# Two layers of a vision network on one core: the last gate moved ahead of the gather, four factors kept in PSUM, and the residual addition given to GpSimd

## The chip, the core and the metric

The kernel runs on one core of a Trainium2 chip. A core has five engines that run their own instruction streams in order and wait for one another through semaphores: TensorE (PE: matrix products and transposes, from SBUF into PSUM), VectorE (DVE), ScalarE (ACT), GpSimd (POOL) and SyncE (SP, which here issues most DMA transfers). SBUF holds the operands, 128 partitions wide; PSUM holds the results of PE in eight banks of 512 float32 columns. Everything is float32.

The metric is the device time of one execution in microseconds (us), lower is better. Times stand for one profiled execution, or for the median of separate runs, and the text says which.

## The reference

The input x is 4 x 48 x 48 x 128 (images, height, width, channels). Two layers run one after the other, each as `x = x + layer(group_norm(x))`.

```python
# layer 0: four scan directions over the 2304 pixels of an image
xz = einsum('bhwc,ec->bhwe', x, in_proj_w); xin, z = split(xz, 2)
xc = silu(depthwise_conv3x3(xin) + conv_b)
xs = stack([x0, x1, x0[..., ::-1], x1[..., ::-1]])     # rows, columns, and both reversed
dt = softplus(dts + dt_proj_b)
h = h * exp(dt_l * A) + (dt_l * u_l) * B_l             # a scan over pixels, 16 states
y = einsum('bkdn,bkn->bkd', h, C_l)
y = (sum of the four directions + Ds * xs)
y = (y - mean(y)) * rsqrt(var(y) + 1e-5) * norm_g + norm_b
out = einsum('bhwd,cd->bhwc', y * silu(z), out_proj_w)

# layer 1: attention and two spectral convolutions over "images" of 48 x 128
xa_n = _inorm(xa)
k, q, v = _fno_layer(xa_n, ...) three times            # rfft2, weights on low modes, irfft2, plus a scaled skip
out = softmax(q k^T / sqrt(d)) v ; projd = _fno_layer(out, wP, ...)
attention = _inorm(projd + xa)
an = _inorm(attention)
m = gelu(_inorm(spec_conv(an, wM0)) + skip(an))
m = _inorm(spec_conv(m, wM1)) + skip(m)
output = _inorm(m) + attention
```

`_inorm` subtracts the mean of an image and divides by its standard deviation. `group_norm` does so over groups of four channels.

## The kernel before

**Order.** Nearly all compute operations are issued through a helper, `Ordered`, that keeps the order of the program on each engine; so they all have line L55 in the profile, and groups are told apart by tile names. Transfers are issued by SP in program order. Code that belongs beside other code is written as Python generators that are advanced piece by piece: where a generator yields, something else is issued.

**Layer 0** (`first_layer`) goes through images 0 to 3, through four directions each, through five chunks each (four of 480 pixels, one of 384), and through 16 steps per chunk, one for each state. A step scans on VectorE (`h`), multiplies by C on GpSimd (`hc`) and sums on PE (`yp`). `put_away` runs when a step's sums are through; after a chunk's last step (`u.i == N - 1`) it copies the sums (`turned`) and queues a `gather`, which adds the directions (`pg`, into `yb`) and queues `back` for the chunk (L487 to L561). `back` is a chain: mean `pm`, subtraction, `Square` on ScalarE, `pv` on PE, a power -0.5 on GpSimd (`var`), transpose `pe`, factor `rs`; then the gate, two products `pz` with two ScalarE operations each and one product on VectorE giving silu(z) (kept in `z`); then `yb *= z` on GpSimd, projection `po`, times `rs`, a second projection `pr` of z with the input added, and the final sum. For the last chunk (image 3, pixels 0 to 479) the result goes straight into `x_in[1]`, the copy of images 2 and 3 that layer 1 reads.

**Between the layers**, that last `back` runs in turn with `opening` (L1131 to L1194): pieces of the one, then pieces of the other. `opening` loads layer 1's constants and x_in (seven transfers, L1161), and for images 0 and 1 (pair 0, still in SBUF as `x_0`) takes statistics (`measure`, which is BATCH_NORM_STATS), the scale and shift (`affine`, with two small PE products and a power on GpSimd), the `means`, the forward spectra along the width (`forward_w`: twelve products `pa`, evacuated in turn by VectorE and ScalarE) and the variances (`squares`, with `pv`, to the factor `in_r`). Once the last chunk is there ("done"), it takes the last statistics and the scale of pair 1 (images 2 and 3). Pair 1's means and spectra come in the gather phase of layer 1 (L1437 to L1446).

**Layer 1's last part** works on two `Strand`s (L1875 to L2245), strand 0 for images 0 and 1, strand 1 for images 2 and 3; y is the strand's 48 rows of 128 x 96 (attention), m the same for the two spectral convolutions. Each strand has main phases p0 to p5 and tails t0 to t5. The loop at the end issues p0(strand 0), p0(strand 1), p1(strand 0) and so on, and with each step of a phase two steps of the tail of the phase before it, which is one of the other strand. What matters here:

- p2: spectra along the height (`e_m`), stored to DRAM; beside them GpSimd computes `m = y * sw`, six operations of 768 columns a strand (the profile calls y `xa`).
- t2: loads the spectra back (`load_e2`, L1932), sums, and the factor `t3 = rsqrt(...) * s2`: a Sqrt on ScalarE, a reciprocal and the product `t<-t,s` on VectorE.
- p3: in each pair of steps `e_m *= t3`, then inverse transforms on PE (`pi_m`), `m += pi_m`, GELU and Square on ScalarE, sums on PE into the tile `st`; GpSimd computes `y *= s1` (`xa<-xa,s`), six of 768 columns.
- p4: spectra again, their squares on ScalarE and products `ce = e * a2` on VectorE, both summed on PE; GpSimd adds the input to y (`xa<-xa,xr`).
- t4: the factors `v5`, `s5`, `qe`, `qm` on vectors of 96 columns (t, v, d, s, sw in the profile).
- p5: `e_m *= qe`, then `skip`: `m *= qm` and `m += y`, two operations each of 768 columns; then `pi_m` on PE and `m += pi_m`; then `put`: transposes on PE (`pf`), a copy with bias on ScalarE (`ot`) and the store. `put(t - 1)` is issued in step t, `put(5)` in t5.

Each strand's sums tile `st` is a PSUM bank opened anew in phases p1 to p4 (`open_sums`); sums fill 384 of its 512 columns. All the factors are tiles of 96 columns in SBUF.

Of the kernel before, what the change touches and what calls it, by code (L numbers as in the profile page):

```python
# [10 lines left out]
F32 = mybir.dt.float32  # L11
BF16 = mybir.dt.bfloat16
AF = mybir.ActivationFunctionType
# [45 lines left out]
def first_layer(ctx, tc, io, x1_dram, sp_dram, d_w, d_m, opening):  # L59
# [426 lines left out]

    def back(b, s, n, yb, x, w, wb):  # L487
# [70 lines left out]
        if b == B - 1 and s == 0:  # L558
            to = images[b]["x1"][:, 1].rearrange("w h t -> w (h t)")[:, 0:n]
# [158 lines left out]
    def gather(c, yt):  # L718

        k, s, n = c.k, c.s, c.n  # L720
        final = k == ORDER[-1]
        if final:
            yb = two.tile([128, NF, LC], F32, tag="yb", name=f"yb{c.t}")
        elif "y" not in c.im:
            c.im["y"] = one.tile([128, NF, L], F32, tag="y", name=f"y{c.b}")
        for f in range(NF):
            p = side(f"pg{c.t}_{f}")
            if final:
                w, v = ident, c.im["y"][:, f, s : s + n]
            else:  # L730
                w, v = ddiag[:, f], c.im["xc"][:, f, s : s + n]
            for j, t in enumerate((yt, c.old)):
                for q, r in blocks(n):
                    on.tensor.matmul(
                        p[:, q * LB : q * LB + r],
                        t[0:r, q, f * 128 : (f + 1) * 128],
                        ident[0:r, 0:r],
                        start=(j == 0 and q == 0),
                        stop=False,
                        is_transpose=True,  # L740
                        skip_group_check=True,
                    )
            on.tensor.matmul(p[:, 0:n], w, v, start=False, stop=True, skip_group_check=True)
            yield
            if final:
                on.scalar.copy(yb[:, f, 0:n], p[:, 0:n])
            else:
                on.scalar.copy(at(c.im["y"], 1, s, n)[:, f], like(p[:, 0:n], 1))
            if f == 0:
                yield FREE  # L750
        if c.next:
            recall(c.next)
        if final:
            backs.append(back(c.b, s, n, yb, c.im["x"], c.im["w"], c.im["wb"]))
            later.append(backs[-1])

    def put_away(u):

        c, n = u.c, u.c.n
        if u.i < N - 1:  # L760
            return
# [29 lines left out]
    later, backs, gathers, projected = deque(), deque(), deque(), deque()  # L791
# [190 lines left out]
def layer1(ctx, tc, io, x1_dram, out):  # L982
# [78 lines left out]
    def spread(psum, p, t, name, aff=None):  # L1061

        v = small.tile([128, T], F32, tag="in_s", name=f"in_{name}{p}")
        on.vector.tensor_reduce(v, t[:, 0 : HB * T].rearrange("p (h t) -> p t h", t=T), AX.X, ALU.add)
        o = psum.tile([128, 512], F32, tag="st", name=f"po_{name}{p}")
        for b in range(2):
            ob = o[:, b * T : (b + 1) * T]
            on.tensor.matmul(ob, g_of[:, b], v, start=True, stop=aff is None)
            if aff is not None:
                on.tensor.matmul(ob, aff[:, 1, b : b + 1].to_broadcast([128, 128]), over_w, start=False, stop=True)  # L1070
        return o

    def means(psum, p, x, aff):
# [3 lines left out]
        pm = psum.tile([128, 512], F32, tag="st", name=f"pm{p}")  # L1077
# [10 lines left out]
        om = spread(psum, p, pm, "m", aff)  # L1088
# [42 lines left out]
    def opening(stack, x_0, last):  # L1131
# [31 lines left out]
        measure(0, 0, x_0, range(6))  # L1163
        yield
        measure(0, 1, x_0, range(6))
        yield
        made["aff"] = [affine(psum, 0)]
        yield
        trans = forward_w(psum, work, 0, x_0, made["aff"][0])
        norm = means(psum, 0, x_0, made["aff"][0])  # L1170
        for _ in range(3):
            next(norm)
            yield
        made["m"] = next(norm)
# [5 lines left out]
        for i in range(5):  # L1180
            next(rest)
            yield
            if i == 1:
                measure(1, 0, x_in[1], range(6))
        made["r"] = [next(rest)]
        measure(1, 1, x_in[1], range(2, 6))
        over_h = const.tile([H, H], F32, name="over_h")
        nc.gpsimd.memset(over_h, 1.0 / H)
        ident = load("ident1", [128, 128], io["c_ident"])
        fh = load("fh", [96, 96], io["c_FH"])  # L1190
        while "done" not in last:
            yield
        measure(1, 1, x_in[1], range(2))
        made["aff"].append(affine(psum, 1))  # L1194
# [193 lines left out]
    with ExitStack() as ph:  # L1388
# [51 lines left out]
        norm = means(psst, 1, x_in[1], aff[1])  # L1440
        trans = forward_w(psum, work, 1, x_in[1], aff[1])
        for _ in range(3):
            next(norm)
        next(trans)
        m = next(norm)
        mine = squares(psst, work, 1, x_in[1], aff[1], m)  # L1446
# [429 lines left out]
    class Strand:  # L1876


        def __init__(self, p):
            self.p = p  # L1880
            self.y = xa[:, :, p * P : p * P + P]
            self.m = None
            self.e2 = {}

        def bank(self, name):
            return psum.tile([128, 512], F32, tag="mm", name=f"{name}_{self.p}")

        def open_sums(self, name):
            self.st = psst.tile([128, 512], F32, tag=f"st{self.p}", name=f"st_{name}_{self.p}")
# [25 lines left out]
        def rsqrt(self, name, v, bias, scale=1.0):  # L1915
            r = self.vector(name)
            on.scalar.activation(r, v, AF.Sqrt, bias=bias, scale=scale)
            on.vector.reciprocal(r, r)
            return r
# [29 lines left out]
        def along_h(self, name, fill, more=None, beside=None):  # L1949
            self.de = dram.tile([2, H, 32, P], F32, name=f"de_{name}_{self.p}")  # L1950
            self.wait = []
            for k in range(0, 32, 4):
# [6 lines left out]
                on.scalar.copy(e[:, k % 8 : k % 8 + 4], images(b[0:96]))  # L1959
                if k % 8 == 4:  # L1960
# [7 lines left out]
        def product(self, e, other, k0, name):  # L1968
            t = self.blk("ap", [128, 8, P], f"{name}{k0}", 4)[0:96]
            if other is None:  # L1970
                on.scalar.activation(t, e, AF.Square)
            else:
                on.vector.tensor_mul(t, e, other)
# [53 lines left out]
        def p1(self):  # L2027

            self.open_sums("y")
# [35 lines left out]
        def p2(self):  # L2065

            self.m = imgs.tile([128, H, P], F32, tag=f"p{self.p}", name=f"m_{self.p}")
            self.open_sums("m0")
# [5 lines left out]
            def more(e, k0):  # L2074
                n = k0 // 8
                t = self.product(e, None, k0, "sqe0")
# [9 lines left out]
        def t2(self):  # L2086
# [6 lines left out]
            self.t3 = self.rsqrt("t3", self.s22, eps)  # L2093
# [3 lines left out]
        def p3(self):  # L2097

            self.open_sums("g")
# [39 lines left out]
        def p4(self):  # L2139

            self.open_sums("m1")
# [4 lines left out]

            def more(e, k0):
                ts = [self.product(e, None, k0, "sqe1"), self.product(e, self.a2[:, k0 : k0 + 8], k0, "ce1")]
# [13 lines left out]
            yield from self.along_h("m1", fill, more, beside)  # L2162

        def t4(self):
# [9 lines left out]
            v5, u = self.vector("v5"), self.vector("d")  # L2174
# [6 lines left out]
            s5 = self.rsqrt("s5", v5, eps)  # L2181
            self.times(s5, s5, n_g[:, 5:6])
            yield
            self.qe, self.qm = self.vector("t3"), self.vector("sw")
            self.times(self.qm, s5, wsm[1])
            on.vector.tensor_mul(self.qe, t4, s5)
# [19 lines left out]
        def p5(self):  # L2206


            def skip(q):
                for i in range(2):  # L2210
                    v = self.m[:, 24 * i + q : 24 * i + q + 8]
                    on.vector.tensor_mul(v, v, over(self.qm, 8))
                    on.vector.tensor_add(v, v, self.y[:, 24 * i + q : 24 * i + q + 8])

            for t in range(6):
                q = 8 * (t // 2)
                if t % 2 == 0:
                    on.vector.tensor_mul(self.e2[q], self.e2[q], over(self.qe, 8))
                    skip(q)
                for b, h in self.along_w("m1", t):  # L2220
                    v = self.m[:, h : h + QB]
                    on.vector.tensor_add(v, v, images(b))
                if t:
                    self.put(t - 1)
                yield

# [142 lines left out]
```

## Time and profile before

| what | us |
|---|---|
| median of three runs | 4452.84 (4444.05, 4452.84, 4453.03) |
| the profiled execution | 4458.8 |
| its span, first to last instruction | 4457.0 |
| VectorE busy, PE busy | 3865.2 (87%), 3808.3 (85%) |
| ScalarE busy, GpSimd busy | 3440.9 (77%), 3351.2 (75%) |
| mean granted PE clock | 0.947 of full speed |

The span falls into layer 0's scans (to about 3710), the passage between the layers and the attention (to about 4190), and the strands' phases. The following view gives the engines' busy time in six stretches of the span (start:end, length, then busy us of each engine with its number of instructions; PEclk is the granted PE clock, the last two are the share of time that the DMA engines were busy and what they moved):

```profile
0.00:3700.00 3700.00, 3192.94 (x22270) 2619.96 (x22271) 3400.54 (x2115) 3158.00 (x6459) 3025.03 (x3217) 0.96 0.36 101
3700.00:3820.00 120.00, 79.84 (x327) 37.06 (x324) 57.16 (x110) 26.49 (x45) 28.90 (x128) 0.82 0.33 90
4190.00:4290.00 100.00, 87.04 (x531) 56.08 (x530) 19.23 (x46) 43.33 (x93) 20.68 (x26) 0.85 0.51 136
4290.00:4314.00 24.00, 2.67 (x25) 1.78 (x23) 23.93 (x3) 4.29 (x6) 23.60 (x14) 0.63 0.28 77
4314.00:4400.00 86.00, 65.93 (x392) 32.70 (x392) 38.01 (x68) 50.08 (x93) 16.62 (x9) 0.76 0.63 146
4400.00:4457.00 57.00, 33.60 (x166) 19.86 (x166) 45.88 (x65) 18.28 (x32) 6.69 (x3) 0.77 0.47 133
```

The engines stand in the order PE, PE's weight loads, VectorE, ScalarE, GpSimd.

### The profile page before, as it was taken

What the parts mean: (1) busy time and instruction counts of PE and PEld (TensorE: products, weight loads), DVE (VectorE), ACT (ScalarE), POOL (GpSimd) and SP (SyncE); (2) the same over time, 40 slices, a digit from 0 to 9 for tenths busy, and PEclk for the clock granted to TensorE, in tenths of its full rate; (3) what the DMA queues carried; (4) which work ended last, traced back from release to release, by engine and by line L of the source; (5) the groups of instructions that cost most, each with busy time, mean ns of one, the idle gap of its engine ahead of it and who ended that gap; (6) DMA issues with size and microseconds to landing.
All of it is one profiled execution on the core that took longest, in us unless ns stands there. A gap on an engine that the chain in (4) does not pass through costs nothing. (4 is left out here: it accounts for less than half of the span.)

```text
span 4457.0 us, 73318 instructions
## 1 busy us (share of the span) xinstructions
PE 3808.3 (85%) x26040; PEld 2932.0 (66%) x26040; DVE 3865.2 (87%) x2652; ACT 3440.9 (77%) x6963; POOL 3351.2 (75%) x3515
## 2 busy tenths in 40 slices
PE   6989987888899978898999788878887796989866
PEld 3767776777677767776777677766776673534434
DVE  3989899999898999998999999998999995578546
ACT  3888888998788889987888898888999883424344
POOL 2777788988787889887778898887888984258432
PEclk9999999999899999998999999999999998999987
DMA  2333333433333333333333334334333333147536
GB/s 62 92 97 100 96 94 102 115 100 107 97 102 94 94 103 107 107 106 97 102 96 98 100 113 122 108 102 102 104 107 100 107 99 100 51 108 170 131 100 163
DMA packets 327946, 463.13 MB, mean 104 GB/s; under 512 B 112772, under 2 KB 295492, under 8 KB 326876
## 3 DMA queue, kind: packets, MB, share of 16 engines
q1 hardware_dynamic: 313072, 435.81, 35.7%
q10 hardware_dynamic: 14508, 22.64, 1.5%
q8 instruction: 206, 3.38, 0.3%
q14 instruction: 160, 1.31, 0.1%
HBM read 403.10 MB, written 55.44 MB: 103 GB/s over the span
## 5 line engine op out<-in xcount | busy, mean ns | idle before, releaser
L55 POOL TENSOR_TENSOR hc<-h,cbc 128x960 f32<-128x960 f32 (+1 forms) x1280 | 2546.4, 1991 | 563.0 <-PE yp L55 184.0
L55 DVE TENSOR_TENSOR_SCAN h<-da,carry,db 128x962 f32<-128x962 f32 (+1 forms) x640 | 1358.2, 2122 | 114.9 <-ACT da L55 95.5
L55 DVE TENSOR_TENSOR_SCAN h<-decay,carry,da 128x962 f32<-128x962 f32 (+1 forms) x640 | 1365.2, 2133 | 7.0 <-PE da L55 5.5
L55 PE MATMUL yp<-ident,hc 128*128 128x128 f32 (+1 forms) x9728 | 1263.2, 282 | 57.0 <-POOL hc L55 53.4
L55 PEld LDWEIGHTS yp<-ident,hc 128*128 128x128 f32 (+1 forms) x9728 | 1133.6, 144 | 222.8 <-issue 110.2
L55 ACT ACTIVATE scaled<-turned,bt 128x256 f32<-128x256 f32 (+1 forms) x2432 | 1037.2, 499 | 28.3 <-ACT turned L55 23.6
L55 ACT ACTIVATE da<-dt,a_neg 128x480 f32<-128x480 f32 (+1 forms) x1280 | 826.9, 646 | 187.3 <-DVE h L55 164.5
L55 ACT ACTIVATE decay<-dt,a_neg 128x480 f32<-128x480 f32 (+1 forms) x1280 | 800.2, 675 | 28.4 <-DVE h L55 23.9
L55 PE MATMUL da<-ident,scaled 128*128 128x128 f32 (+1 forms) x4864 | 647.2, 276 | 196.4 <-DVE h L55 180.8
L55 DVE TENSOR_TENSOR db<-du,pb 128x960 f32<-128x960 f32 (+1 forms) x640 | 701.3, 1096 | 110.4 <-PE pb L55 100.6
L55 PEld LDWEIGHTS da<-ident,scaled 128*128 128x128 f32 (+1 forms) x4864 | 544.3, 145 | 245.6 <-ACT scaled L55 100.0
L55 PE MATMUL pb<-ident,bt 128*128 128x128 f32 (+1 forms) x2432 | 375.7, 276 | 37.2 <-DVE db L55 37.1
L55 PEld LDWEIGHTS pb<-ident,bt 128*128 128x128 f32 (+1 forms) x2432 | 292.2, 141 | 169.3 <-issue 98.9
L55 PE MATMUL pc<-pad,w_c 128*128 128x480 f32 (+1 forms) x720 | 336.5, 582 | 6.5 <-ACT th L55 3.0
L55 POOL TENSOR_TENSOR du<-dt,xc 128x480 f32<-128x480 f32 (+1 forms) x160 | 206.3, 1290 | 49.9 <-ACT dt L55 49.9
L1769 PE MATMUL acc<-v,attn_c 128*64 128x384 f32 x1152 | 203.0, 492 | 9.1 <-DVE v L1751 5.4
L55 PEld LDWEIGHTS da<-carry,ident 128*128 128x128 f32 x1280 | 201.6, 199 | 0.0
L55 PE MATMUL da<-carry,ident 128*128 128x2 f32 x1280 | 197.7, 224 | 0.0
L55 POOL COPY carry<-h 128x2 f32<-128x2 f32 x1024 | 194.3, 190 | 0.0
L1753 POOL TENSOR_TENSOR v<-grep,xrep 128x768 f32<-128x768 f32 x88 | 162.7, 1852 | 35.1 <-PE acc L1769 23.3
L55 PE MATMUL pd<-xd,w_dt 40*128 40x480 f32 (+1 forms) x320 | 172.1, 619 | 16.7 <-ACT bt L55 7.8
L1751 DVE TENSOR_TENSOR v<-gp,xrep 128x1536 f32<-128x1536 f32 x88 | 153.7, 1754 | 27.6 <-PE acc L1769 12.4
(395 smaller groups left out, 3863.5 us busy)
## 6 DMA issues: line engine op xcount, KB each, us to landing
cbc<-cd SPq DMA_DIRECT2D x512, 240.0 KB
cbc<-other SPq DMA_DIRECT2D x512, 240.0 KB
xrep<-dxt SPq DMA_DIRECT2D x44, 576.0 KB
cbc<-cd SPq DMA_DIRECT2D x128, 192.0 KB
cbc<-other SPq DMA_DIRECT2D x128, 192.0 KB
yt<-turned ACTq DMA_DIRECT2D x40, 384.0 KB
old<-yt SPq DMA_DIRECT2D x40, 384.0 KB
grep<-dgt SPq DMA_DIRECT2D x16, 576.0 KB
```

Source lines behind the costliest of these rows:

```text
L55: return lambda *args, **kw: self._tc.keep_in_program_order(emit(*args, **kw))
L1751: nc.vector.tensor_mul(v, gp[:, None, :, 0:NC].to_broadcast([128, 2, 2, NC]), x[:, :, 0:2])
L1753: nc.gpsimd.tensor_mul(v3, r[:, 2:3].to_broadcast([128, 2, NC]), x[:, :, 2])
L1769: nc.tensor.matmul(acc[c][64 * b : 64 * b + 64, 0:NC], attn_c[:, 2 * pair + b, g, q], v[:, b, c] if c < 2 else v3[:, b], start=first, stop ...
```

## The change

It has three parts.

1. **The last gate, and the scale of images 2 and 3.** A new generator `gate` computes silu(z) of the last chunk by itself. It is queued four steps before the end of the last chunk (after any `back` still open is finished) and finished before the sums of the last step are copied. `last_back` then replaces `back` for this chunk: `Square` goes to a tile of its own, so that `yb *= z` on GpSimd (two operations of 480 columns) is issued right beside it; `pr` and `po` have PSUM tiles of their own and are issued ahead of `pe`. In `opening`, the statistics of images 2 and 3 are taken during the means of pair 0; scale and means of pair 1 are issued as soon as the last chunk is there, in turn with pair 0's spectra (`first_pair` holds pair 0's steps). The loads of `ident` and `fh` and the memset of `over_h` move to the end of `opening`.
2. **Factors in PSUM.** Each strand has one tile `st` for all its phases, and its columns 384 to 479 are `tv`. The factors `t3`, `v5`, `s5` and `qm` are in `tv`; `qe` stays in SBUF. In p4 the products `ce` are taken four rows at a time, from the PSUM bank that holds the spectra, instead of eight rows at a time from their copy in SBUF.
3. **p5.** `e_m *= qe` (`grade`) and `m *= qm` (`skip`) are issued earlier, the addition of y is made per 384 columns after `m += pi_m`, on GpSimd, except in the last step, where VectorE makes it; `put` comes one step later (`put(t - 2)`), with `put(4)` behind the loop.

```diff
@@ put_away: the gate in the last chunk
+        if c.final and c.b == B - 1 and c.k == ORDER[-1]:
+            if u.i == N - 4:
+                while backs:
+                    drain(backs.popleft())
+                c.im["gate"] = []
+                gates.append(gate(c.b, c.s, n, c.im["x"], c.im["w"], c.im["wb"], c.im["gate"]))
+                later.append(gates[-1])
+            if u.i == N - 1:
+                drain(gates.pop())
@@ new: gate, last_back (their cores)
+        on.gpsimd.tensor_copy(like(xp, 1), at(x, 1, s, n)[:, 0])
+        for f in range(NF):
+            pz = side(f"pz{t}_{f}")
+            on.tensor.matmul(pz[:, 0:n], w[:, f * 128 : (f + 1) * 128], xp, start=True, stop=True)
+            yield
+            bias = wb[:, f : f + 1]
+            on.scalar.activation(z[:, f, 0:n], pz[:, 0:n], AF.Identity, bias=bias, scale=0.5)
+            on.scalar.activation(th[:, f, 0:n], pz[:, 0:n], AF.Tanh, bias=bias, scale=0.5)
+            yield FREE
+        on.vector.scalar_tensor_tensor(z[:, :, 0:n], th[:, :, 0:n], 1.0, z[:, :, 0:n], ALU.add, ALU.mult)
...
+        on.scalar.activation(sq[:, :, 0:n], ys, AF.Square)
+        for f in range(NF):
+            on.gpsimd.tensor_mul(ys[:, f], ys[:, f], z[:, f, 0:n])
...
+        pr = ps_b.tile([128, 512], F32, tag="pb", name=f"pr{t}")
...
+        po = ps_y.tile([128, 512], F32, tag="yp0", name=f"po{t}")
...
+        on.vector.tensor_mul(xo[:, 0:n], po[:, 0:n], rs[:, 0:n])
+        to = images[b]["x1"][:, 1].rearrange("w h t -> w (h t)")[:, s : s + n]
+        on.vector.tensor_add(to, xo[:, 0:n], pr[:, 0:n])
@@ opening
         made["aff"] = [affine(psum, 0)]
-        yield
+        pair_0 = first_pair(psum, work, x_0)
+        while next(pair_0, last) is not last and "done" not in last:
+            yield
+        while "done" not in last:
+            yield
+        measure(1, 1, x_in[1], range(2))
+        made["aff"].append(affine(psum, 1))
+        norm = means(psum, 1, x_in[1], made["aff"][1], "pp")
+        for _ in range(3):
+            next(norm)
+            next(pair_0, None)
+        made["m1"] = next(norm)
+        for _ in pair_0:
+            pass
+        over_h = const.tile([H, H], F32, name="over_h")
+        nc.gpsimd.memset(over_h, 1.0 / H)
+        ident = load("ident1", [128, 128], io["c_ident"])
+        fh = load("fh", [96, 96], io["c_FH"])
@@ Strand
+            self.st = psst.tile([128, 512], F32, tag=f"st{p}", name=f"st_{p}")
+            self.tv = self.st[:, QB * P : QB * P + P]
...
-            self.t3 = self.rsqrt("t3", self.s22, eps)
+            self.t3 = self.rsqrt("t3", self.s22, eps, to=self.tv)
             on.vector.tensor_mul(self.t3, self.t3, self.s2)
...
+                v = cross[k0][:, j : j + 4]
+                on.vector.tensor_mul(v, images(b[0:96]), self.a2[:, k : k + 4])
...
-            v5, u = self.vector("v5"), self.vector("d")
+            v5, u = self.tv, self.vector("d")
...
-            s5 = self.rsqrt("s5", v5, eps)
+            s5 = self.rsqrt("s5", v5, eps, to=self.tv)
...
-            self.qe, self.qm = self.vector("t3"), self.vector("sw")
+            self.qe, self.qm = self.vector("t3"), self.tv
@@ p5
+            def grade(q):
+                on.vector.tensor_mul(self.e2[q], self.e2[q], over(self.qe, 8))
             def skip(q):
                 for i in range(2):
                     v = self.m[:, 24 * i + q : 24 * i + q + 8]
                     on.vector.tensor_mul(v, v, over(self.qm, 8))
-                    on.vector.tensor_add(v, v, self.y[:, 24 * i + q : 24 * i + q + 8])
+            grade(0)
+            skip(0)
             for t in range(6):
-                q = 8 * (t // 2)
-                if t % 2 == 0:
-                    on.vector.tensor_mul(self.e2[q], self.e2[q], over(self.qe, 8))
-                    skip(q)
-                for b, h in self.along_w("m1", t):
+                made = self.along_w("m1", t)
+                if t == 1:
+                    grade(16)
+                    skip(8)
+                if t == 3:
+                    skip(16)
+                for b, h in made:
                     v = self.m[:, h : h + QB]
                     on.vector.tensor_add(v, v, images(b))
-                if t:
-                    self.put(t - 1)
+                    add = on.vector if t == 5 else on.gpsimd
+                    add.tensor_add(v, v, self.y[:, h : h + QB])
+                if t == 0:
+                    grade(8)
+                if t > 1:
+                    self.put(t - 2)
                 yield
+            self.put(4)
```

## The prediction

> **What bounds the kernel now.** I read the page first: over the span VectorE is busy 87%, PE 85%, ScalarE 77%, GpSimd 75%, so the average names nobody. By stretches it does: up to 3700 us VectorE works 3400.5 us of 3700 (the scans), and the change leaves that stretch alone but for its last steps. After it (3700 to 4457) no engine is full, and waits decide. The chain of waits through the last 300 us has one link that stands out (start, us, what):
>
> ```profile
> 4282.20 3.95 PE pe_m L55 x24
> 4290.63 23.10 DVE t L55
> 4314.81 1.63 PE pi_m L55 x3
> ```
>
> One VectorE instruction on 96 columns holds the chain for 23 us. The timeline around it (start, length, engine, operation, in brackets the idle time before and who ended it):
>
> ```profile
> 4289.84 0.75 DVE L55 RECIPROCAL t<-t 128x96 f32<-128x96 f32 x1 [1.47 <-ACT t L55]
> ...
> 4290.63 23.09 DVE L55 TENSOR_TENSOR t<-t,s 128x96 f32<-128x96 f32 x1
> ...
> 4292.43 21.17 POOL L55 TENSOR_TENSOR xa<-xa,s 128x768 f32<-128x768 f32 x12
> ...
> 4313.75 0.96 DVE L55 TENSOR_TENSOR e_m<-e_m,t 128x768 f32<-128x768 f32 x1
> ...
> 4314.81 1.74 PE L55 MATMUL pi_m<-e_m,iw 64*128 64x384 f32 x4 [22.14 <-DVE e_m L55]
> ```
>
> It starts behind a GpSimd operation and ends 0.1 us after the last of an unbroken row of them (4292.43 + 21.17 = 4313.60); PE then waited 22.14 us. The groups of 4190 to 4457, shapes kept apart, and below them, by itself, a row of 3000 to 3700 (columns: busy us, mean ns of one, idle before):
>
> ```profile
> L55 DVE TENSOR_TENSOR t<-t,s 128x96 f32<-128x96 f32 x4 | 23.9, 5966 | 1.0 <-ACT s L55 0.9
> ...
> L55 DVE TENSOR_TENSOR v<-v,d 128x96 f32<-128x96 f32 x2 | 1.9, 964 | 1.2 <-ACT d L55 1.1
> L55 DVE TENSOR_TENSOR m<-m,xa 128x768 f32<-128x768 f32 x12 | 13.0, 1085 | 1.2
> L55 DVE TENSOR_TENSOR m<-m,sw 128x768 f32<-128x768 f32 x12 | 13.0, 1084 | 0.0
> L55 POOL TENSOR_TENSOR xa<-xa,xr 128x768 f32<-128x768 f32 x12 | 23.3, 1946 | 73.3 <-DMA xr<-x 73.3
> ```
>
> ```profile
> L55 DVE TENSOR_TENSOR db<-du,pb 128x960 f32<-128x960 f32 x96 | 108.9, 1134 | 10.6 <-PE pb L55 10.6
> ```
>
> The other three t<-t,s take 0.26 us each, the second v<-v,d too (0.26 against 1.67 for the first, which has GpSimd's xa<-xa,xr beside it). All of these read two operands from SBUF. db<-du,pb has one operand in PSUM: 128x960 in 1.13 us through 700 us in which GpSimd multiplies nearly all the time. So a VectorE operation with two SBUF operands is held while GpSimd works, and one with an operand in PSUM is not. The last phase shows it again, on a smaller scale (two GpSimd operations, from 4402.40 and 4404.16; each VectorE operation ends its own 0.8 to 0.9 after the end of one):
>
> ```profile
> 4402.40 4.28 POOL L55 TENSOR_TENSOR xa<-xa,xr 128x768 f32<-128x768 f32 x2 [2.51 <-DMA xr<-x]
> ...
> 4402.55 2.47 DVE L55 TENSOR_TENSOR m<-m,xa 128x768 f32<-128x768 f32 x1
> 4404.94 2.55 DVE L55 TENSOR_TENSOR m<-m,sw 128x768 f32<-128x768 f32 x1
> 4407.60 0.96 DVE L55 TENSOR_TENSOR m<-m,xa 128x768 f32<-128x768 f32 x1
> ```
>
> Between the layers, images 2 and 3 begin only when images 0 and 1 are done:
>
> ```profile
> 3776.11 2.86 DVE L55 BATCH_NORM_STATS2 st<-x_in 128x6 f32<-128x384 f32 x6
> ...
> 3784.65 0.16 DVE L55 TENSOR_TENSOR aff<-gmean_l,aff 128x2 f32<-128x2 f32 x1 [2.81 <-POOL aff L55]
> ...
> 3785.14 4.14 PE L55 MATMUL pm<-x_in,a_m 128*32 128x384 f32 x24 [3.50 <-DVE a_m L55]
> ...
> 3789.45 2.19 PE L55 MATMUL pa<-x_in,fwa 128*66 128x384 f32 x4
> ```
>
> **The change, part A: last gate and scale.** The 13.3 us from 3776.11 to 3789.45 go: statistics, scale and means of images 2 and 3 move into the spectra of images 0 and 1 (3738.9 to 3761). What comes in their place: (1) the gate now stands ahead of the last two steps' sums on PE: copy xp on GpSimd (1.03 us, delays the last hc by 0.4), first pz 1.0, its two ScalarE operations 1.2 before the second pz may reuse the bank, second pz 1.1. The sums ended at 3710.6; they would end near 3713.5, +2.9, and all behind them (gather, norm, scale of image 0) with them. (2) The scale chain of images 2 and 3 (3778.9 to 3785.1, 6.3 us with its trips to PE and GpSimd) stands on VectorE in program order between the first and the second evacuation of the spectra, and the spectra wait for it: +6.3. (3) Their means, 4.1 us on PE, stand ahead of the second: +4.1. (4) Out of that stretch fall the old last projections, po 3.4, pr 1.0 + 1.8: -6.2 of PE, because they run with banks of their own before it (the x_in sum, at 3753.99 now, then comes by about 3739). Sum -13.3 + 2.9 + 6.3 + 4.1 - 6.2 = **-6.2**. On SP the seven x_in loads now stand behind seven weight loads (ident to fw, 0.3 to 0.6 us each, some 4 us), and VectorE's statistics of image 2 stand ahead of the last image's final sum; the loads now run until about 3725 and would until 3729, when the statistics are due: free if so. Ends: -12.6, if (2) and (3) hide in the waits between evacuations (1.9 to 2.5 us each) but for the 4.0 that PE can't hide; +2, if (4) saves nothing because po and pr already lay in such waits, and the loads come 2 late.
>
> **Part B: t3 in PSUM.** The 23.09 us product has one operand in PSUM and should take 0.26. What is late next is the load of the first spectra (SP's issues from 4288.72, four per group, about 2 us to land): about 4293.2; p3 could start near 4294 instead of 4313.75, **-20**. GpSimd's row still ends at 4313.6, and until then p3 now runs beside it: its VectorE operations (e_m times t3, m plus pi_m, copies of pa_m) all have an operand in PSUM. What GpSimd writes there is needed in p4, some 50 us on. Ends: -23, if the shorter idle also spares PE part of its lower clock (0.63 granted in that window, 0.85 in the 100 us before); -15, if p3 runs beside GpSimd by some 10% slower and each product waits for the sums that share t3's bank (a new wait of PE on the third product, some 1.0 us of st sums).
>
> **Part C: p4.** The first v<-v,d falls from 1.67 to 0.26, -1.4; eight products of 0.97 become sixteen of half the size at about 0.5 (as m<-m,pi_m, 548 ns), now straight from PSUM, and the bank is held until both ScalarE's copy and the product are through, 0.5 us more with PE the bound: **-1.5** with ends -2.5 and +1 (one held bank in each strand).
>
> **Part D: p5.** VectorE's part now takes 19.9 us a strand (4431.81 to 4451.7). Ten of twelve additions of 384 columns go to GpSimd: 3 x 0.88 (grades) + 6 x 0.88 (skips) + 12 x 0.47 + 2 x 0.48 = 14.5, so -5.3 in the second strand, and in the first -5.3 and the 3.1 of stretch at 4402 to 4407. GpSimd's ten take about 0.95 each (768 columns: 1.81 when undisturbed), 9.5 a strand, under VectorE's time; but in the first strand they queue behind the second strand's xr additions (last one to 4410.2), and PE's transposes, put off by one step, wait for them: that gives about 4421 for its end instead of 4424.6. The t4 chain of strand 1 (4424.56 to 4431.81) no longer stands behind full VectorE steps, -3. Against it: one more put behind the loop, PE 1.9, on the path at the end; three grades per strand with both operands in SBUF, each held until GpSimd's row runs dry, 0.5 if that is one addition, more where a row has queued up. Sum -3.6 - 3 - 5.3 + 1.9 = -10.0; the grades I put at nothing, since nothing waits for a grade until the phase's next pair of steps: **-10**. Ends -14 (strand 0 gains all 8.4) and -3 (strand 0 gains nothing, grades and put some 2 us a strand dearer).
>
> A page speaks against part B. The Trainium skill, "SBUF — State Buffer", section "SBUF: two separate sides", says that VectorE with two SBUF inputs and GpSimd share a port pair under a lock, held by whichever starts first for the whole instruction. The kind of operand agrees with the rows, and so does the length at 4402 (one operation each); the length at 4290 does not: held for one instruction, the product would have waited some 1.8 us, not 23.09 past a row of twelve. By the page the rest has another cause; that is rival 3.
>
> Sum: -6.2 - 20 - 1.5 - 10 = -37.7. Against the profiled span 4457.0 this is 4419.3 (that run took 4458.8: 4421.1). The median is 4452.84, 6 below the profiled run; the stalls are in every run, so **4415**.
>
> **Rivals.** (1) GpSimd binds p5: its additions behind the xr sums delay transposes and output as much as VectorE gains; for it, xr waits for DMA 73.3 us in all; against, only strand 0 overlaps. D gives 0: 4425. (2) B moves the wait: loads, the bank shared with sums, or ScalarE's GELU table make p3 start late or run slower; for it, PE's next work needs four loads; against, the first load has landed by 4293.2 and is not waited for at 4313. B gives 8 to 10: 4426. (3) The 23 us is not GpSimd's hold but a wait written down so; PSUM spares one GpSimd operation, 1.6: 4452.8 - 6.2 - 1.6 - 1.5 - 10 = 4433.5. Against: the product and v<-v,d (4394.67) end 0.1 us after a GpSimd operation (4313.61 and 4394.55), and the product's inputs were there at 4290.6. (4) Slower: GpSimd holds VectorE wherever the operand is, because result and other operand are in SBUF. Then B and C give 0, and each of the 20 new additions holds VectorE for its 0.95: +19, +3.8 for two more puts, -8.8 for additions moved (20 x 0.44), -6.2 for A: 4461. It decides once the hold covers some 60% of the additions (11.2 of 19). Against: db<-du,pb at 1.13 beside GpSimd. (5) B, C and D are given back whole in a later wait for DMA (the xr and spectra loads share queues), and A alone stays: 4447. For it, the chain has DMA links of 2 to 3 us in the last 80 us; against, no link of it is a load that was issued early and came late.
>
> **How the numbers follow.** Forecast 0.62, rivals (1) 0.12, (2) 0.10, (3) 0.05, (4) 0.07, (5) 0.04. All low ends together give 4401, all high ends 4438; the range 4400 to 4438 holds these and rivals 1 to 3, and leaves out (4), (5) and what lies beyond the bounds. What a measurement can't tell from no change is 0.2%, 8.9 us: faster 0.87 (the forecast and rivals 1 to 3, less 0.02 for their own tails), same 0.06 (rival 5 and those tails), slower 0.07 (rival 4).
>
> **What would show it.** Right: t<-t,s (or its PSUM name) at 0.26 everywhere, the first p3 product near 4294 less A's gain while GpSimd still multiplies, PE idle there under 3 us; images 2 and 3's first pa some 6 us earlier; p5 of the second strand under 15 us on VectorE, GpSimd's additions near 0.95. Wrong: a PSUM-operand product stretched to GpSimd's end (4), a wait on DMA, PE or ACT of over 10 us ahead of p3 (2), transposes waiting on GpSimd through p5 (1), or x_in's statistics waiting for DMA ahead of the last sum.

## The result and the profile after

| | before | changed |
|---|---|---|
| median of four runs, us | 4451.43 (4444.05 to 4453.03) | 4421.09 (4418.83 to 4429.0) |
| ratio, 95% interval | | 0.994 (0.9918 to 0.9963) |
| a second chip session | 4455.55 (23 runs) | 4429.88 (9 runs), ratio 0.995 (0.9933 to 0.9967) |
| span of the profiled execution | 4457.0 | 4417.0 |

The change makes the kernel 0.4 to 0.8% faster by the first ratio, 30 us by the first medians and 26 by the second, where 37.7 was forecast. The two profiled spans differ by 40 us, and 13.4 of that can't be credited to the change: the last scan starts at 3705.04 before and at 3691.59 after, and in the fourteen profiles of this study it starts anywhere from 3689 to 3711, whatever the kernel (on average at 3698 in the five with the old layer 0, at 3701 in the nine with the changed one). So everything below is measured in stages that leave the scans out. Their limits are starts of instructions in the timelines: the last scan (S), the first t3 product (T), the first e_m product of p5 in strand 0 (L0) and in strand 1 (L1), and the end (E).

| us | S to T | T to L0 | L0 to L1 | L1 to E | S to E |
|---|---|---|---|---|---|
| before | 585.6 | 110.0 | 31.2 | 25.2 | 752.0 |
| changed | 582.1 | 91.3 | 28.9 | 23.1 | 725.4 |
| changed, again (e5) | 589.4 | 89.9 | 30.9 | 23.1 | 733.2 |

S to T holds the attention, which varies by itself (585.6 to 589.3 in the five profiles with the old passage between the layers); a nearer mark for part A is the last evacuation of images 2 and 3's spectra, 105.4 after S in all five of these, and 100.0 to 103.7 in the five with the changed passage (after and e4, e5, e9, e10).

The stall is gone. The changed kernel's timeline at the place of the 23.09 us product (`st` is the PSUM tile that now holds t3):

```profile
4273.05 21.32 POOL L55 TENSOR_TENSOR xa<-xa,s 128x768 f32<-128x768 f32 x12
...
4273.70 0.27 DVE L55 TENSOR_TENSOR st<-st,s 128x96 f32<-128x96 f32 x1
4276.44 0.95 DVE L55 TENSOR_TENSOR e_m<-e_m,st 128x768 f32<-128x768 f32 x1 [2.48 <-DMA e_m<-de_m]
4280.95 1.02 DVE L55 TENSOR_TENSOR m<-m,pi_m 128x384 f32<-128x384 f32 x2 [3.55 <-PE pi_m L55]
```

GpSimd's row is as long as before, and three kinds of VectorE operation, each with one operand in PSUM, pass beside it at their own length. What is late now is the load of the spectra, for 2.48 us. The groups of 4150 to 4417 (busy, mean ns, idle before):

```profile
L55 DVE TENSOR_TENSOR m<-m,st 128x768 f32<-128x768 f32 x12 | 10.8, 942 | 0.0
...
L55 DVE TENSOR_TENSOR e_m<-e_m,t 128x768 f32<-128x768 f32 x6 | 8.6, 1455 | 0.0
...
L55 DVE TENSOR_TENSOR e_m<-e_m,st 128x768 f32<-128x768 f32 x6 | 5.7, 946 | 2.5 <-DMA e_m<-de_m 2.5
```

The same product on the same shape takes 946 ns with its factor in PSUM (t3, p3) and 1455 with its factor in SBUF (qe, p5); m times qm fell from 1084 to 942. The additions on GpSimd and what they wait for:

```profile
L55 POOL TENSOR_TENSOR xa<-xa,xr 128x768 f32<-128x768 f32 x12 | 23.7, 1973 | 58.6 <-DMA xr<-x 57.5 <-DVE m L55 1.1
...
L55 POOL TENSOR_TENSOR m<-m,xa 128x384 f32<-128x384 f32 x20 | 20.4, 1055 | 14.1 <-DVE m L55 14.1
```

In the last phase of strand 0 they come late, behind the other strand's xr additions, and the wait goes round from GpSimd to PE to VectorE:

```profile
4374.80 1.81 POOL L55 TENSOR_TENSOR xa<-xa,xr 128x768 f32<-128x768 f32 x1 [1.09 <-DVE m L55]
...
4376.56 5.77 POOL L55 TENSOR_TENSOR m<-m,xa 128x384 f32<-128x384 f32 x6
4377.61 2.04 PE L55 MATMUL pf<-ident,m 128*96 128x128 f32 x8 [6.20 <-POOL m L55]
...
4382.54 0.55 DVE L55 TENSOR_TENSOR m<-m,pi_m 128x384 f32<-128x384 f32 x1 [5.18 <-PE pi_m L55]
```

Between the layers two operations that the forecast did not count stand in the way (`ACTq` is ScalarE's queue, here issuing a load):

```profile
3696.02 1.17 ACTq L1308 DMA_DIRECT2D iw<-in_c_IW  x2
3697.29 1.21 ACT L55 ACTIVATE ws<-pz,wb 128x480 f32<-128x480 f32 x2 [11.64 <-POOL mean_m L55]
...
3741.32 0.16 DVE L1387 TENSOR_TENSOR wpv<-wpv 128x4 f32<-128x4 f32 x1 [3.83 <-DMA mask<-in_c_ident]
```

The first pz ended at 3694.93, but ScalarE's queue held the issue of a constant's load, `iw`, ahead of the gate, and that starts only at 3696.02, just after GpSimd's last hc had ended (3695.99). And VectorE, in the middle of the second scale chain, waited for a load that a tiny product of attention weights needs: both are issued without the helper that keeps program order, and stand where the scheduler (the software that orders what the program leaves free) put them.

### The profile page after: what moved, and what is told of

Read it like the earlier page. It is cut to its first block, busy times and chain, and to the rows that moved or that the text cites. A ratio compares the mean times of both kernels' runs of the same rounds, so it can differ in the third digit from the quotient of the medians.

```text
span 4417.0 us, 73366 instructions
## 1 busy us (share of the span) xinstructions
PE 3799.2 (86%) x26040; PEld 2920.9 (66%) x26040; DVE 3833.6 (87%) x2652; ACT 3436.6 (78%) x6963; POOL 3376.8 (76%) x3536
## 4 chain that ended last, share of the span: by engine, by line
PE 35%; DVE 23%; ACT 22%; issue 12%; POOL 4%; DMA 3%; SPq 1%; ACTq 0%; POOLq 0%; DVEq 0%
DVE h L55 14%; PE yp L55 8%; ACT scaled L55 6%; DVE db L55 5%; PE pc L55 5%; ACT da L55 4%; PE da L55 4%; ACT decay L55 4%; PE pd L55 2%; ACT dt L55 2%; PE acc L1859 2%; POOL hc L55 2%; ACT turned L55 2%; PE pg L55 2%; PE pb L55 2%
## 5 line engine op out<-in xcount | busy, mean ns | idle before, releaser
L55 PE MATMUL pb<-ident,bt 128*128 128x128 f32 (+1 forms) x2432 | 373.8, 275 | 37.7 <-DVE db L55 37.7
L1843 POOL TENSOR_TENSOR v<-grep,xrep 128x768 f32<-128x768 f32 x88 | 162.3, 1847 | 35.0 <-PE acc L1859 21.5
```

The costliest lines, as they stand in the source:

```text
L55: return lambda *args, **kw: self._tc.keep_in_program_order(emit(*args, **kw))
L1843: nc.gpsimd.tensor_mul(v3, r[:, 2:3].to_broadcast([128, 2, NC]), x[:, :, 2])
```

## The experiments

**e1: t3 alone in PSUM**, in the kernel before.

```diff
+            self.st = psst.tile([128, 512], F32, tag=f"st{p}", name=f"st_{p}")
+            self.tv = self.st[:, QB * P : QB * P + P]
...
-            self.t3 = self.rsqrt("t3", self.s22, eps)
+            self.t3 = self.rsqrt("t3", self.s22, eps, to=self.tv)
```

> The kernel before with t3 alone in PSUM (product and result), nothing else changed. Measured by stages, which leave the scans out: from the start of the t3 product of the first strand to the first e_m product of its last phase, before 110.0 us, changed kernel 91.3; from there to the end of the span, 56.4 and 52.0. Theory (GpSimd holds VectorE operations with two SBUF operands): product 0.27 instead of 23.1, the first stage 91 to 92, the last unchanged at 56 to 57, the whole some 18 to 20 us shorter. Rival, the 23 us is another wait: product 21 or more wherever its operand lies, some 1.6 us gained. Rival, GpSimd holds it whatever memory: nothing gained.

Its product and the operation behind it in the timeline:

```profile
4291.52 0.27 DVE L55 TENSOR_TENSOR st<-st,s 128x96 f32<-128x96 f32 x1
4294.54 0.95 DVE L55 TENSOR_TENSOR e_m<-e_m,st 128x768 f32<-128x768 f32 x1 [2.76 <-DMA e_m<-de_m]
```

T to L0 is 91.3, as in the whole change, and L0 to E 57.8. The ratio to before is 0.9971 (0.9955 to 0.9986), 6 to 20 us. Both rivals fall: this part alone brings 18.7 us of the stage. The whole change brings 18.8 to 26.6 off S to E in its two profiles, so t3 is the larger part of it; by the ratios (0.29% against 0.5 to 0.6%) it is about half, with wide intervals.

**e2: one operand in PSUM, the result in SBUF.** As in e1 the reciprocal goes to `tv`; the product does not:

```diff
-            on.vector.tensor_mul(self.t3, self.t3, self.s2)
+            t3 = self.vector("t3r")
+            on.vector.tensor_mul(t3, self.t3, self.s2)
+            self.t3 = t3
```

> The kernel before with the reciprocal in PSUM, so that the t3 product reads one operand there, but its result in SBUF as before. Theory (each VectorE operation with two SBUF operands is held while GpSimd's row runs): the product takes 0.27, and the next operation, e_m<-e_m,t with both operands in SBUF, is held in its place until the row ends, some 20 us; the stage from the product to the last phase stays near 110 us. Rival, the wait belongs to the product alone (or to its vector of 96 columns): the stage falls to 91 or 92.

```profile
4290.36 0.26 DVE L55 TENSOR_TENSOR t3r<-st,s 128x96 f32<-128x96 f32 x1
...
4290.38 21.19 POOL L55 TENSOR_TENSOR xa<-xa,s 128x768 f32<-128x768 f32 x12
...
4293.56 18.83 DVE L55 TENSOR_TENSOR e_m<-e_m,t3r 128x768 f32<-128x768 f32 x1 [2.94 <-DMA e_m<-de_m]
```

The product passes though its result lies in SBUF, and the next operation with two SBUF operands is held in its place, to 4312.39; GpSimd's row ended at 4311.57, and 0.8 later the product was through. T to L0 is 107.6. So the two inputs decide, not where the result goes, and it is no property of the vector of 96 columns.

**e3: pauses in GpSimd's row**, all factors in SBUF.

```diff
                 on.gpsimd.tensor_mul(v, v, over(self.s1, 8))
+                pace = self.vector("pace")
+                on.gpsimd.tensor_copy(pace[:, 0:1], sq[:, 0, 0:1])
```

> The kernel before, all factors in SBUF, with a copy of one column on GpSimd behind each xa<-xa,s that waits for the square of that step, so that the row of twelve has pauses. Theory (the hold lasts as long as GpSimd goes from one operation to the next without a pause): the product is through at the first pause, behind the first xa<-xa,s, 3.5 to 4 us instead of 23.1; the stage of 110 us falls to 91 to 96, since later products wait for at most one GpSimd operation. Rival, held for one instruction only: under 2 us. Rival, no hold by GpSimd: 23 us as before.

```profile
4276.17 1.80 POOL L55 TENSOR_TENSOR xa<-xa,s 128x768 f32<-128x768 f32 x1
4287.23 0.19 POOL L55 COPY pace<-sqm 128x1 f32<-128x1 f32 x1 [9.27 <-ACT sqm L55]
```

```profile
4276.48 1.60 DVE L55 TENSOR_TENSOR t<-t,s 128x96 f32<-128x96 f32 x1
```

The product ends 0.1 us after the first xa operation, at the first pause; T to L0 is 95.7, 14.3 less than before with no factor in PSUM. My 3.5 to 4 us missed, and 1.60 is the number that the rival of one instruction gave: GpSimd was further on when the product came, so here it met a single operation, and this run by itself cannot tell a hold of one operation from a hold of a row. Together with e2, where ten operations in a row held one product, it can: there the hold outlasts single operations, and here it ends at the pause, long before GpSimd's work does.

**e4: the addition of y on VectorE again.**

```diff
-                    add = on.vector if t == 5 else on.gpsimd
+                    add = on.vector
```

> The changed kernel with all additions of y in the last phase on VectorE again, the order otherwise as changed. From the first e_m product of the last phase to the end: before 56.4, changed 52.0. Theory (in the first strand GpSimd's additions stand behind xr and PE's transposes wait for them, which gives back most of the 5.3 us a strand): 51 to 55 us, PE's wait of 6.2 us ahead of its first transposes under 3. Rival, VectorE's time bounds the last phase as forecast: 60 us (52 and twice 10 additions of 0.47 less what was hidden).

L0 to L1 is 29.0 (28.9 and 30.9 with GpSimd's additions), L1 to E 25.5 (23.1), together 54.5, as expected. PE's wait for GpSimd is gone. So giving the addition to GpSimd brings nothing in strand 0 that this one profile can show, and 2.4 us in strand 1, where L1 to E is 25.2 to 25.7 in the four profiles with the old p5.

**e5 to e8: the changed kernel again; without part A; with the two operations of part A out of the way; and with qe in PSUM besides.** e6 joins the old text up to the strands with the changed strands. e7 and e8:

```diff
-        nc.vector.tensor_mul(wpv[:, 0], wpv[:, 0], wpv[:, 1])
+        on.vector.tensor_mul(wpv[:, 0], wpv[:, 0], wpv[:, 1])
...
-        nc.scalar.dma_start(iw2[64 * i : 64 * i + 64], io["c_IW"])
+        nc.sync.dma_start(iw2[64 * i : 64 * i + 64], io["c_IW"])
... e8 only
-            self.qe, self.qm = self.vector("t3"), self.tv
+            self.qe, self.qm = self.st[:, 0:P], self.tv
```

> The changed kernel again, on the same chip as the next three. From the start of the last scan to the t3 product: before 585.6 us, changed 582.1; from the product to the last phase 110.0 and 91.3; from there to the end 56.4 and 52.0. Theory (the stages are fixed and the 13 us that the profiled run gained in the scans are spread between executions): these three repeat within 1 us, and the time is 25 to 30 us below before. Rival, the gate or the longer program moves the scans: the start of the last scan is again some 13 us earlier than before's on average.

> The changed kernel without the first part: layer 0, the passage between the layers and the attention as before, the strands as changed. Theory (the first part brings 3.5 us): last scan to t3 product 585 to 586, the other stages as changed (91, 52), time 3 to 4 us above the changed kernel. As forecast: 6.2 above. Rival, the first part moves the scans: 10 us or more above.

> The changed kernel with two operations kept from standing in the way of its first part: the small product wpv in program order on VectorE (it stood in the middle of the second scale chain and waited 3.8 us for the mask's load), and the loads of iw issued by SP instead of ScalarE (they stood ahead of the gate's ScalarE operations and waited for the scans' memory, 2.4 us). Theory: the last scan to the t3 product falls from 582.1 by 4 to 6 us, and the gate's first ScalarE operation starts within 0.2 us of its product. Rival, something else is late there (loads, the variances): under 2 us.

> As the run before, and qe in PSUM too (in columns of the sums tile that are free by then), so that the products e_m times qe have one operand there. Theory (these are held by GpSimd's additions: two of them take 3.4 and 3.3 us where 1.8 would do): two take 1.8 in both strands, and the last phase to the end falls from 52.0 by 1.5 to 3 us; the time is some 6 to 9 us below the changed kernel. Rival, the last phase of the second strand is bound by GpSimd and PE: nothing from qe.

| | ratio to before | last evacuation after S | L0 to E | S to E |
|---|---|---|---|---|
| e5 | 0.9950 (0.9933 to 0.9967) | 103.6 | 54.0 | 733.2 |
| e6 | 0.9954 (0.9936 to 0.9971) | 105.4 | 52.0 | 731.5 |
| e7 | 0.9933 (0.9907 to 0.9959) | 96.4 | 54.0 | 724.9 |
| e8 | 0.9935 (0.9914 to 0.9957) | 92.1 | 49.8 | 718.6 |

In times these four can't be told apart: single executions spread over 19 to 29 us, and the start of the last scan alone over 22 in the profiles. e5's scans began their last step at 3701.87, and by the averages above the changed kernel starts it no earlier: the rival of e5 and e6 (13 or 10 us) is not borne out, though e5's own claim that the stages repeat within 1 us was wrong in all three (by 7.3, 1.4 and 2.0), and e6's S to T, 588.1, lies above the 585 to 586 expected. By its nearer mark part A brings 1.7 to 5.4 us. In e7 the gate's ScalarE operation no longer waits behind the load:

```profile
3702.51 1.07 PE L55 MATMUL pz<-xp,w 128*128 128x480 f32 x2 [1.22 <-POOL xp L55]
...
3703.62 1.21 ACT L55 ACTIVATE ws<-pz,wb 128x480 f32<-128x480 f32 x2 [8.74 <-PE pz L55]
```

The sums now end 7.9 us after S instead of 11.7 to 12.6 (before 5.5); the last evacuation comes 3.5 to 11.6 earlier in e7 and e8 than in the changed kernel's profiles. The predicted fall of S to T itself (4 to 6 us) does not show in e7 alone (582.5 against 582.1 and 589.4); it does in e8 (578.9). With e11 and e12, which have the same two mends, the four take 577.2 to 582.5, 579 on average, against 581.7 to 589.4, 585.5 on average, in the five without.

e7 and e8 have the same instructions in that passage and still differ by 4.3 us. One group shows why (e7, then e8):

```profile
3726.62 3.33 PE L55 MATMUL pr<-ws,w_out 128*128 128x480 f32 x4
```

```profile
3735.95 1.77 PE L55 MATMUL pr<-ws,w_out 128*128 128x480 f32 x4
```

Each of the four products took 934 to 1007 ns in e7 and 566 or 567 in e8, with no wait between them; the granted PE clock over these stretches was 0.53 and 1.00. This group accounts for 1.6 of the 4.3 us, and three later ones (two pa, one pm) for 1.8 more. Over the first 38 us after S the granted clock was 0.85 and 0.89, and over the 45 us behind them 0.75 and 0.82. So this passage varies by some us with the clock, and a gain of that size there needs several profiles.

qe does what was expected; in e8's timeline:

```profile
4381.59 1.81 DVE L55 TENSOR_TENSOR e_m<-e_m,st 128x768 f32<-128x768 f32 x2
...
4409.66 1.81 DVE L55 TENSOR_TENSOR e_m<-e_m,st 128x768 f32<-128x768 f32 x2
```

In the changed kernel's profile such a pair took 3.43 and 3.25 us. In strand 1 that repeats (3.25 in e7); in strand 0 it depends on where GpSimd stands, since e5 and e7 have 1.82 there with qe in SBUF. So the effect is shown in strand 1, where L1 to E falls from 23.1 to 21.8 (and to 21.5 to 21.7 in e11 and e12). The 6 to 9 us of time that e8 expected below the changed kernel are not shown: the medians differ by 5.8, and the intervals overlap.

**e9: four buffers for xr.**

```diff
-                    xr = self.blk("xr", [128, 8, P], f"xr{q}", 2)
+                    xr = self.blk("xr", [128, 8, P], f"xr{q}", 4)
```

> The changed kernel with four buffers for xr instead of two. In the changed kernel SP waited 6.4 us in all for GpSimd to free one, and so held back the loads behind it; GpSimd's last xr addition ended 11.6 us after the last phase of the first strand began, and only then came its first additions of that phase, for which PE waited 6.2 us. From the first e_m product of the last phase to that of the second strand: before 31.2, changed 28.9 to 30.9. Theory (the queue of xr additions binds the last phase of the first strand): GpSimd ends them 3 us or more earlier in the phase, PE's wait falls below 3, the stage to 25 to 27 us. Rival, the loads themselves (or the t4 chain behind them) bind it: within 1 us of 28.9.

L0 to L1 is 28.3; GpSimd ended the xr additions 10.4 us after L0 instead of 11.6, and PE's wait was 3.3. SP's wait for buffers fell from 6.4 us to 0.7, but the additions end hardly sooner: the rival holds. Nor is PE's shorter wait surely due to the buffers: e6 with two has 4.0, e11 with four 6.6.

**e10: ce from SBUF again**, whole in `more` instead of by halves in `each`.

```diff
...
-                on.vector.tensor_mul(v, images(b[0:96]), self.a2[:, k : k + 4])
+                on.vector.tensor_mul(v, e, self.a2[:, k0 : k0 + 8])
```

> The changed kernel with the ce products from SBUF again, eight rows at a time. From the first e_m product of p3 to that of p5: before 86.9, t3 alone in PSUM 88.2, changed 88.5 and 87.3. Theory (ce from PSUM costs nothing and brings nothing; the rest of what was forecast for p4 was one held product): 86 to 89. Rival, sixteen products straight from PSUM hold the banks and cost 1.5 or more: under 86.

From p3's first product to L0 it is 85.3, against 85.9 to 88.9 (mean 87.5) in the seven profiles with ce from PSUM and two xr buffers. By its number this is the rival's side, under 86; but the seven spread over 3.0 us, and one profile lies 0.6 below the nearest of them. With four xr buffers the same stage takes 88.3 (e9) and 83.2 (e11) with ce from PSUM, so 85.3 shows no cost of it. The eight products took 1276 ns each (969 in the kernel before), 10.2 us in all; the sixteen take 8.6, and no gain of that shows in the stage. Whether holding the banks costs a microsecond or two stays open.

**e11: the mends of e8 with four buffers for xr. e12: the mends of e8 with the tail t4 taken faster.**

```diff
-                next(tail, None)
-                next(tail, None)
+                for _ in range(6 if main.__name__ == "p5" else 2):
+                    next(tail, None)
```

> The changed kernel with all the mends together: wpv in order, iw issued by SP, qe in PSUM, four buffers for xr. Theory: from the last scan to the last evacuation of images 2 and 3's spectra 92 to 97 us (changed 100.7 to 103.7), the last phase to the end 46 to 50 (52 to 54), the time 8 to 14 us below the changed kernel's, ratio to before near 0.992. Rival, xr brings nothing: as with the first three alone, 49.8 in the last phase and a ratio of 0.9935.

> The changed kernel with wpv in order, iw issued by SP and qe in PSUM, and beside the last phase of the first strand six steps of the other strand's tail t4 with each step instead of two, so that its sums stand ahead of the first transposes on PE (which wait for GpSimd's additions) and its factors are worked out while those wait. From the first e_m product of the last phase to that of the second strand: before 30.9 to 32.7, changed 28.9 to 31.2, with the three mends alone 28.1. Theory (the t4 chain behind the first strand's transposes sets when the second strand starts): 23 to 26 us, the last phase to the end 45 to 48 us. Rival, the loads of the second strand's spectra or GpSimd's additions bind: within 1.5 us of 28.1. Against the kernel before the ratio would be near 0.992 or 0.993.

e11: ratio 0.9924 (0.9898 to 0.9949), last evacuation 92.1, L0 to E 50.6, S to E 715.0. Its ratio is the one expected, but the last phase is not: 50.6 lies beside the rival's 49.8, so four buffers brought nothing there. e12: ratio 0.9929 (0.9907 to 0.9952), L0 to L1 29.4, L0 to E 50.9: a miss. Its timeline on PE shows that the chain moved and did not get shorter:

```profile
4385.55 2.04 PE L55 MATMUL pf<-ident,m 128*96 128x128 f32 x8 [3.91 <-POOL m L55]
4387.39 1.01 PE L55 MATMUL tot_m<-red,g 128*128 128x96 f32 x4
4393.87 0.44 PE L55 MATMUL pbias<-one,mu 1*96 1x1 f32 x2 [5.47 <-DVE mu L55]
```

The sums now pass, but the totals still stand behind transposes that wait for GpSimd, and the chain of factors, which VectorE and ScalarE pass to and fro, now holds up strand 0's own steps behind it. So in e12 strand 0's last phase waits for GpSimd's additions behind xr, and then for this chain. Which of the two sets its length in general is not shown: without GpSimd's additions (e4) it is as long, with more work on VectorE.

e8, e11 and e12, like the changed kernel, are faster than the kernel before (their intervals lie below 1), and from the last scan to the end they take 715 to 720 us, where four profiles of the changed kernel or its like (after, e5, e9 and e10) take 724 to 733. That they beat the changed kernel in time is not shown: the intervals of the ratios overlap.

## Why the prediction held, and where its sizes were off

The time forecast was 4415, the medians are 4421 and 4430, within the range. By the time alone the forecast can't be told from its rivals 1 and 2 (4425 and 4426), which lie as near; what decides is the stages. Part B, over half of the sum, came out by its mechanism; the other parts came out smaller than their sizes, all on the same side, which is why 26 to 30 us were gained instead of 37.7. Of the signs named, the product at 0.27 and p3 running beside GpSimd's row came out. The second strand's p5 under 15 us on VectorE did not (17.6, from 4393.91 to 4411.49), nor the first pa of images 2 and 3 some 6 us earlier (0 to 3 after S in the five profiles), and transposes waiting for GpSimd, the sign of rival 1, are there in strand 0 (6.20). Term by term:

- **Part B, -20: right, and by its mechanism.** From the start of the product to p3's first e_m product 23.1 became 2.7, -20.4; the next late thing was the load, as said. T to L0 gives back 1.7 of it; in the timeline pi_m now waits behind PE's last products of the other strand's p2 (the 3.55 above). Rivals 2 and 5, by which a later wait gives B back, are out by the 18.7 us of e1. Rival 3, by which PSUM spares one GpSimd operation and no more (4433.5), is out by e1, and e2 shows the long hold again. The Trainium skill, "SBUF — State Buffer", section "SBUF: two separate sides", has the shared port pair held for one whole instruction; e1 and e2 agree with it in which operands matter, and e2's 18.83 us, ten operations long, differ in the length, where the measurement decides. The slower rival, that GpSimd holds VectorE whatever the memory, is out by e1, and by the 946 ns beside a full row of GpSimd.
- **Part A, -6.2: 1.7 to 5.4 measured.** The gate was to delay the sums by 2.9; they end 6.2 to 7.1 later after S than before, and 2.4 later in e7. Mis-sized was the wait between the first product and ScalarE: only the operations that the diff adds were counted, not what already stood in ScalarE's queue. In the same way the second scale chain, put at 6.3, took 8.0 from the last statistics to the first pm, 3.8 of it the wait for wpv; in e7 it took 4.2. Both are shown by e7, where these waits are gone: with the two mends the last evacuation comes 9.0 to 13.3 earlier than before (e7, e8, e11, e12), more than the 6.2 forecast.
- **Part C, -1.5: not found.** The held product did fall to 0.27, but from p3 to L0 the seven profiles take 87.5 on average, before 86.9 and e1, without part C, 88.2; no gain can be told from their spread of 3.0.
- **Part D, -10: about -4**, the largest error. L0 to E is 56.1 to 57.8 in four profiles with the old p5 and 51.3 to 54.3 in six with the changed one. In strand 0 rival 1 was right that VectorE's gain is lost: GpSimd's late additions make PE wait, e4 shows that without them the stage is the same, and the t4 chain, counted as hidden for 3 us, still stands ahead of L1 (e12). In strand 1, 5.3 was forecast from VectorE's busy time and 2.1 came; two terms that I set at nothing are part of it: the grades held by the additions (1.4; e8 gets 1.3 back) and the last two additions on VectorE (1.06 and 0.70 instead of 0.55 each, beside GpSimd's).

## What to carry to other kernels

When a small VectorE operation takes many times its usual length, look whether GpSimd works through that time without a pause: if both inputs lie in SBUF, put one into a free corner of PSUM, or give GpSimd's row a pause; e1 and e3 show 18.7 and 14.3 us of one stage for a change of a few lines. Whoever moves work to GpSimd should first see what GpSimd has ahead of it at that moment, and which operations of VectorE with two SBUF inputs will then be held by the new work. And where a step is put ahead, look at each engine's queue for operations outside the hand-written order, as they may come to stand inside it (here 2.4 and 3.8 us of waiting).

## What was not expected of the hardware

The hold has two lengths. A row of GpSimd operations that wait for nothing held one VectorE operation through ten of them and more (23.09 us before, 18.83 in e2). In the changed p5, where each addition of GpSimd needs a result of VectorE, the two engines took turns operation by operation, though the second addition's input was there in time:

```profile
4397.31 2.67 POOL L55 TENSOR_TENSOR m<-m,xa 128x384 f32<-128x384 f32 x2 [9.48 <-DVE m L55]
```

```profile
4397.54 3.25 DVE L55 TENSOR_TENSOR e_m<-e_m,t 128x768 f32<-128x768 f32 x2
```

Two additions take 1.96 us undisturbed and 2.67 here, two products 1.82 (e5) and 3.25: each engine waits for the other. In e4, without GpSimd's additions, strand 1's pair is back at 1.82. That a GpSimd operation which carries a wait of its own lets VectorE in, even if the wait is already over, would fit both lengths; it was not tried by itself, so what ends a hold stays open beyond the pause that e3 shows.
